# A second level of Strassen's algorithm in q, k and v, later sums of reciprocals, and another order of the output projection

## The chip, the core and the metric

The kernel runs on one core of a Trainium2 chip. The metric is the device time of one execution in microseconds (us), from runs of the compiled program; beside it stands one execution recorded by the hardware profiler. The engines are called by the profile's names: PE (TensorE, matmuls), PEld (its weight loads), DVE (VectorE), ACT (ScalarE), POOL (GpSimd) and SP (SyncE, which here issues the transfers).

## What is computed

Two graph layers over 64 items of 256 nodes with 512 features, all in float32. Layer 0 multiplies by the adjacency matrix and a weight; layer 1 is attention with 8 heads of 64 in which the adjacency matrix acts as a mask. Names and shapes of the arguments are shortened here:

```python
def setup_inputs(seed=0):
    x = -0.0003929 + 0.9999 * jax.random.normal(..., (64, 256, 512), jnp.float32)
    # adj [256, 256] f32: symmetric pattern with ones on the diagonal, times uniform(0.05, 1)

def _layernorm(x, axis=-1, eps=1e-5):
    m = jnp.mean(x, axis=axis, keepdims=True)
    v = jnp.var(x, axis=axis, keepdims=True)
    return (x - m) / jnp.sqrt(v + eps)

def reference(x, adj, L0_gnn_weight, L0_gnn_bias, Wq, bq, Wk, bk, Wv, bv, Wo, bo):
    h = jnp.maximum(_layernorm(x), 0.0)                       # layer 0
    y = jnp.einsum('nm,bmd->bnd', adj, h)
    x = x + jnp.einsum('bnd,do->bno', y, L0_gnn_weight) + L0_gnn_bias
    h = jnp.maximum(_layernorm(x), 0.0)                       # layer 1
    q = (h @ Wq + bq).reshape(b, n, 8, 64)                    # k and v alike
    scores = jnp.einsum('bqhd,bkhd->bhqk', q, k) / jnp.sqrt(64.)
    scores = scores + (1.0 - adj)[None, None, :, :] * -1000000000.0
    attn = jax.nn.softmax(scores, axis=-1)
    out = jnp.einsum('bhqk,bkhd->bqhd', attn, v).reshape(b, n, 512)
    return x + out @ Wo + bo
```

## The kernel before

**Groups and layers.** The 64 items are worked in 32 groups of two (GB = 2). Layer 0 runs over all groups first and leaves residual and hidden state in DRAM; layer 1 then runs over all groups again. Its steady loop has two halves per group g. First half: attention of heads 0 to 3 (`attend(g, 0)`), the scores of heads 4 to 7 (`score(g, 1)`), then the projections q and k of group g+1 (`queries_keys`). Second half: `attend(g, 1)`, `score(g+1, 0)`, then v of group g+1 (`values`) and the output projection of group g (`post`).

**Products.** Every projection has a weight of 512 x 512 and uses one level of Strassen's algorithm in Winograd's form, in `project`: seven products instead of eight, each of a 256 x 256 weight quarter and 256 tokens. The left factors are weight quarters a11, a12, a22 and prepared sums s1 to s4; the right factors are quarters b11, b21, b22 of the activations and their differences t1 to t4 (`Halves`, written by POOL). The products are called P1 = a11·b11, P2 = a12·b21, P3 = s4·b22, P4 = a22·t4, P5 = s1·t1, P6 = s2·t2, P7 = s3·t3. `product` (L439) issues four matmuls of 128 x 128 weights with 256 columns for each; where the activations are the weights (`by_token`, for v and o) the two sides are swapped. P1, P6 and P7 add up in one PSUM bank (a), P5 and P3 in another (c); between two products ACT (q, k, v) or DVE (o) reads the partial sum (`read`). P2 and P4 have banks of their own (b, d). A `finish` is one DVE addition of a bank and a partial sum (L493). The order is P1 P2 P6 P5 P7 P4 P3, and for the output projection of the last group P1 P5 P2 P6 P7 P4 P3. The partial sums that ACT leaves share three SBUF buffers (`partial`, tag u).

**Order of the work.** The program is written out by hand. Each engine works strictly in the order in which its instructions are written; a `yield` in a projection ends a step, `tick` (L263) counts steps, and `after(n, f)` writes f's instructions n steps later. PSUM has 8 banks, handed out by `bank` in the order in which they were given back (`give`); a bank's next writer waits until its last reader is done.

**Attention.** `score` (L684) makes four pairs of banks with scores, scaled and masked by DVE (L699), then POOL subtracts a maximum (L705), ACT takes the exponent (L710) a few steps later and POOL the sums over pairs of key tiles (L717). `attend` (L719) makes denominators (pden, L726) and weighted values (pav, L733) on PE, ACT copies the denominators (L740), DVE takes four reciprocals of 128 columns (L743) and, one step later in `divide`, multiplies (L750) and gives the banks back; ACT then sums the reciprocals over the free dimension into `stats` (L752), a check for overflow which is evaluated in the last group (L843 to L847). POOL makes the differences of the output projection (L437) in `divide`.

Of the kernel before, what the change touches and what calls it, by code (L numbers as in the profile page):

```python
# [8 lines left out]
F32 = mybir.dt.float32  # L9
# [4 lines left out]
P = 128  # L14
# [184 lines left out]
def kernel(  # L199
# [239 lines left out]
    def product(ps, s, a, halves, b, by_token, start=True, stop=True):  # L439
        for m in range(2):  # L440
            for c in range(2):
                w, y = s[a][:, c, :], halves.operand(b, c)
                lhs, rhs = (y[:, m * P:(m + 1) * P], w) if by_token else (w[:, m * P:(m + 1) * P], y)
                nc.tensor.matmul(ps[:, m, :], lhs, rhs, start=(start and m + c == 0), stop=(c == 1),  # L444
                                 skip_group_check=True)

    def project(s, halves, by_token, name, read, finish, first_half_first=False):


        def new(n):  # L450
            return bank([P, 2, N], f"{name}{n}")
        pa = new("a")
        product(pa, s, "a11", halves, "b11", by_token, stop=False)
        u1 = read(pa, 1)
        yield
        if first_half_first:
            pc = new("c")
            product(pc, s, "s1", halves, "t1", by_token, stop=False)
            c22 = read(pc, 0)
            yield  # L460
        pb = new("b")
        product(pb, s, "a12", halves, "b21", by_token)
        finish(pb, u1, 0, 0)
        give(pb)
# [4 lines left out]
        if not first_half_first:  # L469
            pc = new("c")  # L470
            product(pc, s, "s1", halves, "t1", by_token, stop=False)
            c22 = read(pc, 0)
            yield
        product(pa, s, "s3", halves, "t3", by_token, start=False)
        u3 = read(pa, 3)
        finish(pa, c22, 1, 1)
        give(pa)
        yield
        pd = new("d")
        product(pd, s, "a22", halves, "t4", by_token)  # L480
        finish(pd, u3, 1, 0)
        give(pd)
        yield
        product(pc, s, "s4", halves, "b22", by_token, start=False)
        finish(pc, u2, 0, 1)
        give(pc)
        yield

    def partial(name, n):
# [2 lines left out]
    def add(o, ps, u):  # L492
        nc.vector.tensor_tensor(o, ps, u, op=ALU.add)  # L493
# [125 lines left out]
    def hidden_sums(g, *steps):  # L619

        HH[g] = Halves(f"h_{g}", [H1T[g][:, k] for k in range(GB)], 0 if g else 1)
        for step, n in zip(steps, ("t1", "t2", "t3", "t4")):
            after(step, HH[g].sums, nc.gpsimd, (n,))

    def queries_keys(g):

        for n, store in (("q", Q), ("k", K)):
            store[g] = {}
            bias = L1[n][1]

            def read(ps, m):
                u = partial(f"{n}_{g}", m)
                for c in range(2):
                    f = 2 * (m in (0, 3)) + c
                    nc.scalar.activation(u[:, c, :], ps[:, c, :], AF.Identity, bias=bias[:, f:f + 1])
                return u

            def finish(ps, u, i, k):
                o = store[g][i, k] = act.tile([P, 2, N], F32, tag=f"{n}{i}{k}", name=f"{n}_{g}_{i}{k}")
                add(o, ps, u)  # L640

            yield from project(W[n], HH[g], False, f"{n}_{g}", read, finish)

    def values(g):
        v = act.tile([P, HQ, GB, NT, HF], F32, tag="yT0", name=f"v_{g}")
        V[g] = {(i, k): v[:, i, k] for i in range(HQ) for k in range(GB)}

        def read(ps, m):
            u = partial(f"v_{g}", m)
            nc.scalar.copy(u, ps)  # L650
            return u

        def finish(ps, u, i, k):
            add(V[g][i, k], ps, u)

        yield from project(W["v"], HH.pop(g), True, f"v_{g}", read, finish)

    def quarter_of(batch, i):
        return batch.rearrange("(t p) d -> p t d", p=P)[:, :, i * HF:(i + 1) * HF]
# [59 lines left out]
    def attend(g, qd):  # L719
# [19 lines left out]
        den, rden = dens[:, 0, :], dens[:, 1, :]  # L739
        nc.scalar.activation(den, pd, AF.Identity, accum_out=stats[:, 0, i:i + 1])  # L740
        give(pd)
        for c in range(4):
            nc.vector.reciprocal(rden[:, c * P:(c + 1) * P], den[:, c * P:(c + 1) * P])  # L743
# [140 lines left out]
```

## Time and profile before

| what | us |
|---|---|
| median of 3 runs | 2728.7 (2726.19 to 2729.91) |
| the profiled execution | 2727.19 |
| its span, first to last instruction | 2725.3 |
| one steady group of layer 1 (start of scores to the next, 1845.3 to 1910.25) | 64.95 |

In such a group the engines are busy for 64.95 (PE), 53.45 (PEld), 32.66 (DVE), 19.38 (ACT) and 43.26 us (POOL). The granted clock of PE is 0.998 of the full one over the execution. The page's groups of instructions that the change touches:

```profile
L743 DVE RECIPROCAL den<-den 128x128 f32<-128x128 f32 x256 | 216.8, 909 | 66.9 <-ACT den L740 66.8
L752 ACT ACTIVATE den<-den 128x512 f32<-128x512 f32 x64 | 40.3, 630 | 221.5 <-DVE den L743 221.5
```

A line gives the source line, engine, operation, output and inputs with partitions x elements, and the count; then the busy time in us and the mean of one in ns; then the idle time of the engine in front of them and what ended it. In front of the sums of L752, ACT is idle for 221.5 us in all, and DVE's reciprocals end that. PE's recorded lengths overlap, because matmuls are pipelined; its pace is read from start to start.

### The profile page before, as it was taken

The page shows a single profiled execution, that of the slowest core. Times are in us where ns is not written, and L with a number is a line of the kernel's source. Part 1 is how long each engine was busy: PE and PEld are TensorE (multiplying, and loading weights), DVE is VectorE, ACT ScalarE, POOL GpSimd, SP SyncE. Part 2 cuts the span into 40 slices and gives each one's busy share as a digit, 9 for nine tenths or more (in the row PEclk, how much of TensorE's full clock was granted, in tenths as well). Part 3 has the DMA queues.
Part 4 walks back from the last instruction along what each step waited for, and adds up shares of the span by engine and source line. Part 5 has one row for each costly group of instructions (what it writes and reads, how often), then busy time and mean ns, then how long its engine had stood idle before and what let it go on. Part 6 is the DMA issues. An engine that isn't in the chain of part 4 may idle for free.

```text
span 2725.3 us, 43511 instructions
## 1 busy us (share of the span) xinstructions
PE 2699.5 (99%) x17172; PEld 2252.1 (83%) x17172; DVE 1539.6 (56%) x2781; ACT 874.2 (32%) x1537; POOL 1823.1 (67%) x1426
## 2 busy tenths in 40 slices
PE   8999999999999999999999999999999999999998
PEld 7888888888788888888888888888888888888886
DVE  7877778775444444455554444454555445444556
ACT  3434343443233223222233322222223332223222
POOL 6777776764666666666666666666666666666665
PEclk9999999999999999999999999999999999999999
DMA  7776666664111111111111111111222111111110
GB/s 187 188 193 163 162 168 169 165 153 93 47 47 47 47 47 47 47 47 47 47 47 47 47 47 47 47 47 56 61 62 57 48 47 47 47 47 47 47 47 32
DMA packets 281023, 210.50 MB, mean 77 GB/s; under 512 B 145904, under 2 KB 212976, under 8 KB 280816
## 3 DMA queue, kind: packets, MB, share of 16 engines
q1 hardware_dynamic: 280352, 207.15, 29.2%
q8 instruction: 138, 2.26, 0.4%
q10 hardware_dynamic: 464, 0.52, 0.1%
q14 instruction: 69, 0.57, 0.1%
HBM read 106.96 MB, written 100.66 MB: 76 GB/s over the span
## 4 chain that ended last, share of the span: by engine, by line
PE 98%; POOL 1%; DVE 1%; DMA 0%; issue 0%; ACT 0%; DVEq 0%; ACTq 0%; POOLq 0%
PE sc L694 8%; PE py L539 8%; PE pav L733 8%; PE pden L726 2%; POOL a L705 1%; PE v_31a L444 0%; PE q_31a L444 0%; PE q_27a L444 0%; PE v_22a L444 0%; PE v_18a L444 0%; PE q_18a L444 0%; PE q_14a L444 0%; PE v_9a L444 0%; PE v_5a L444 0%; PE q_5a L444 0%; PE v_30a L444 0%
## 5 line engine op out<-in xcount | busy, mean ns | idle before, releaser
L705 POOL TENSOR_TENSOR a<-a,top 128x1024 f32<-128x1024 f32 x254 | 593.7, 2373 | 699.1 <-DVE a L699 699.1
L699 DVE SCALAR_TENSOR_TENSOR a<-sc,maskT 128x512 f32<-128x512 f32 x512 | 312.1, 683 | 28.5 <-PE sc L694 28.5
L717 POOL TENSOR_TENSOR as<-a 128x512 f32<-128x512 f32 x256 | 317.3, 1277 | 0.7 <-DVE r L575 0.7
L710 ACT ACTIVATE a<-a 128x1024 f32<-128x1024 f32 x256 | 270.8, 1058 | 22.4 <-POOL a L705 22.4
L743 DVE RECIPROCAL den<-den 128x128 f32<-128x128 f32 x256 | 216.8, 909 | 66.9 <-ACT den L740 66.8
L694 PE MATMUL sc<-q,k 64*128 64x256 f32 x2048 | 238.7, 383 | 0.0
L733 PE MATMUL pav<-a,v 128*32 128x256 f32 x4096 | 232.7, 379 | 0.0
L694 PEld LDWEIGHTS sc<-q,k 64*128 64x128 f32 x2048 | 194.4, 187 | 44.9 <-issue 26.3
L539 PE MATMUL py<-adjT,h 128*128 128x256 f32 x1024 | 228.9, 382 | 0.9 <-DVE adjT L325 0.9
L740 ACT ACTIVATE den<-pden 128x512 f32<-128x512 f32 x64 | 38.2, 597 | 581.7 <-PE pden L726 570.6
L539 PEld LDWEIGHTS py<-adjT,h 128*128 128x128 f32 x1024 | 196.1, 192 | 28.7 <-ACT h L514 1.2
L733 PEld LDWEIGHTS pav<-a,v 128*32 128x32 f32 x4096 | 133.1, 110 | 87.9
L569 ACT ACTIVATE h<-x,nb,rs 128x512 f32<-128x512 f32 x128 | 97.1, 806 | 319.0 <-POOL nb L54 319.0
L824 POOL TENSOR_TENSOR x<-x,bo_r 128x512 f32<-128x512 f32 x128 | 159.4, 1283 | 12.9 <-DVE x L493 12.9
L53 POOL TENSOR_TENSOR rs<-rs,mhalf 128x2 f32<-128x2 f32 (+1 forms) x97 | 78.8, 812 | 124.3 <-DVE nb L52 124.2
L518 POOL TENSOR_TENSOR x<-x,b_r 128x512 f32<-128x512 f32 x128 | 159.3, 1280 | 1.0 <-ACT h L514 0.9
L437 POOL TENSOR_TENSOR t_y<-yT,t_y 128x256 f32<-128x256 f32 (+1 forms) x96 | 87.8, 915 | 41.5 <-ACT yT L549 39.0
L752 ACT ACTIVATE den<-den 128x512 f32<-128x512 f32 x64 | 40.3, 630 | 221.5 <-DVE den L743 221.5
L590 DVE BATCH_NORM_STATS2 st<-x 128x6 f32<-128x256 f32 x256 | 96.4, 418 | 4.4
L514 ACT ACTIVATE h<-x,nb,rs 128x512 f32<-128x512 f32 x128 | 93.9, 805 | 10.5 <-POOL nb L54 10.5
L42 DVE BATCH_NORM_STATS2 st<-x 128x6 f32<-128x512 f32 x128 | 85.6, 669 | 7.2 <-DMA x<-in_x_dram 7.2
L437 POOL TENSOR_TENSOR t_y<-yT 128x256 f32<-128x256 f32 (+1 forms) x96 | 87.6, 912 | 2.2 <-ACT yT L549 0.9
(3144 smaller groups left out, 5550.1 us busy)
## 6 DMA issues: line engine op xcount, KB each, us to landing
x<-in_x_dram SPq DMA_DIRECT2D x256, 128.0 KB, 3.5
residual<-x SPq DMA_DIRECT2D x256, 128.0 KB, 2.3
hidden<-r SPq DMA_DIRECT2D x128, 256.0 KB, 4.7
h1T<-hidden SPq DMA_DIRECT2D x64, 512.0 KB, 9.5
x<-residual SPq DMA_DIRECT2D x32, 1024.0 KB, 6.5
out_dram<-x SPq DMA_DIRECT2D x62, 512.0 KB, 3.0
w_sb<-in_L_gnn_weight_dram SPq DMA_DIRECT2D x1, 1024.0 KB, 6.3
wq_sb<-in_L_gnn_Wq_dram SPq DMA_DIRECT2D x1, 1024.0 KB, 6.8
```

The costliest lines, as they stand in the source:

```text
L437: eng.tensor_tensor(self.t[n][:, c, :], self.operand(p, c), self.operand(q, c), op=ALU.subtract)
L518: nc.gpsimd.tensor_tensor(xt[:, t, :], xt[:, t, :], b0_r, op=ALU.add)
L539: nc.tensor.matmul(pss[d][:, b * N:(b + 1) * N], h[:, b * NT + k, d * P:(d + 1) * P], adjT[:, k, :], start=(k == 0), stop=(k == NT - 1))
L569: nc.scalar.activation(h1[:, k * NT + t, :], xt[:, k * NT + t, :], AF.Relu, bias=nb[:, t:t + 1], scale=rs[:, t:t + 1])
L694: nc.tensor.matmul(ps[j][:, kt * N:(kt + 1) * N], k[j * HD:(j + 1) * HD, c, kt * P:(kt + 1) * P], q[j * HD:(j + 1) * HD, c, :], start=True ...
L699: nc.vector.scalar_tensor_tensor(a[:, j * NT:(j + 1) * NT, :].rearrange("p k n -> p (k n)"), ps[j], SCALE, maskT_f, op0=ALU.mult, op1=ALU.add)
L705: nc.gpsimd.tensor_tensor(a, a, top_b, op=ALU.subtract)
L710: nc.scalar.activation(a, a, AF.Exp)
L717: nc.gpsimd.tensor_tensor(AS[c, b], a4[:, :, 0, :], a4[:, :, 1, :], op=ALU.add)
L733: nc.tensor.matmul(po[f][h * 32:(h + 1) * 32, b * N:(b + 1) * N], v[:, k, h * HD + f * 32:h * HD + f * 32 + 32], A[h // 2, b][:, (h % 2) * ...
L743: nc.vector.reciprocal(rden[:, c * P:(c + 1) * P], den[:, c * P:(c + 1) * P])
L824: after(9 + t, lambda t, xt: nc.gpsimd.tensor_tensor(xt[:, t, :], xt[:, t, :], L1["o"][1], op=ALU.add), t, X[g])
```

## The change

**Second level.** For groups 4 to 31 (`FIRST2 = 4`) q, k and v run through the new `project2`. P2, P3 and P4, whose result goes into one quarter of the output only, are split once more: `product2` computes each with seven matmuls of a 128 x 128 weight with 128 columns, four of them into the product's own bank and the common ones into a further bank (`shared`). `finish2` is a list of five DVE operations in place of one addition: own bank plus partial sum, then the shared parts added to 512, 384, 256 and 256 columns of the result (128 in the last, where the product had no earlier content in its bank, `fresh`). P3's and P2's finishes are issued in turn, after P2. The order is P1 P5 P6 P3 P2 P7 P4. P1, P5, P6 and P7 stay as they are.

**Its operands.** `block_sums` forms the sums of the weights' blocks, 12 POOL operations on 128 x 128 for each of q, k and v, in groups 0 to 2, in SBUF that layer 0 no longer needs. `block_hidden` forms the differences of the activations' blocks: six POOL operations per group, issued in the last steps of the second half.

**Reciprocals.** From group 4 on two of the four reciprocals are taken in `attend` and two one step later, at the head of `divide`; in the last `attend` all four stay. The sum of the reciprocals on ACT (`note`) is issued three steps after `divide`, except in the last group.

**Output projection.** It runs for all groups in the order P1 P5 P2 P6 P4 P7 P3 (`in_place=True`); there a partial sum is added to its quarter of x in place, so P4 needs no earlier partial sum. The output's transfers go out after P7 and P3; in the last group they go out by quarters, those that P4 and P7 complete together after P7.

The diff, with blank lines and parts of `project`'s rewritten steps left out:

```diff
@@ project and what is new beside it @@
-    def project(s, halves, by_token, name, read, finish, first_half_first=False):
+    def project(s, halves, by_token, name, read, finish, in_place=False):
+        def p1():
+            o["a"] = new("a")
+            product(o["a"], s, "a11", halves, "b11", by_token, stop=False)
+            o["u1"] = read(o["a"], 1)
...
+        def p3():
+            product(o["c"], s, "s4", halves, "b22", by_token, start=False)
+            finish(o["c"], o["u2"], 0, 1)
+            give(o["c"])
...
+            product(o["a"], s, "s3", halves, "t3", by_token, start=False)
+            o["u3"] = read(o["a"], 3)
+            finish(o["a"], o["c22"], 1, 1)
+            give(o["a"])
+        o = {}
+        for step in (p1, p5, p2, p6, p4, p7, p3) if in_place else (p1, p2, p6, p5, p7, p4, p3):
+            step()
+            yield
+    ONCE = {"a12": "b21", "a22": "t4", "s4": "b22"}
+    FIRST2 = 4
+    W2, spare = {}, []
+    def block_sums(n):
+        todo = []
+        for a in ONCE:
+            w = W[n][a]
+            def part(i, j):
+                return w[:, j, i * P:(i + 1) * P]
+            s1, s2, s3, s4 = (spare.pop(0) for _ in range(4))
+            W2[n, a] = dict(a11=part(0, 0), a12=part(0, 1), a22=part(1, 1), s1=s1, s2=s2, s3=s3, s4=s4)
+            for o, p, q, op in ((s1, part(1, 0), part(1, 1), ALU.add), (s2, s1, part(0, 0), ALU.subtract),
+                                (s3, part(0, 0), part(1, 0), ALU.subtract), (s4, part(0, 1), s2, ALU.subtract)):
+                todo.append((nc.gpsimd.tensor_tensor, o, p, q, op))
+        return todo
+    class Blocks:
+        def __init__(self, x, t):
+            self.x, self.t = x, t
+        def operand(self, n):
+            if n[0] == "t":
+                return self.t[..., {"t1": 0, "t3": 1, "t2": 2, "t4": 3}[n], :]
+            return self.x[..., int(n[1]) - 1, int(n[2]) - 1, :]
+        def sums(self, eng):
+            t, op = self.t, ALU.subtract
+            eng.tensor_tensor(t[..., 0:2, :], self.x[..., :, 1, :], self.x[..., 0, :, :], op=op)
+            eng.tensor_tensor(t[..., 2, :], self.operand("b22"), t[..., 0, :], op=op)
+            eng.tensor_tensor(t[..., 3, :], self.operand("b21"), t[..., 2, :], op=op)
+    def product2(own, shared, s, x, by_token, fresh):
+        q = own.rearrange("p m (n k) -> p (m n) k", k=P)
+        c11, c12, c21, c22 = (q[:, i, :] for i in ((0, 2, 1, 3) if by_token else (0, 1, 2, 3)))
+        for o, a, b, start in ((shared[:, 0, :], "a11", "b11", True), (shared[:, 1, :], "s2", "t2", False),
+                               (shared[:, 2, :], "s3", "t3", False),
+                               (c22 if fresh else shared[:, 3, :], "s1", "t1", fresh),
+                               (c11, "a12", "b21", False), (c12, "s4", "b22", False), (c21, "a22", "t4", False)):
+            lhs, rhs = s[a], x.operand(b)
+            if by_token:
+                lhs, rhs = rhs, lhs
+            nc.tensor.matmul(o, lhs, rhs, start=start, stop=True, skip_group_check=True)
+    def finish2(o, own, shared, u, by_token, fresh):
+        def quarters(t):
+            return t.rearrange("p m (n k) -> p (m n) k", k=P)
+        def spread(i, n):
+            return shared[:, i:i + 1, :].to_broadcast([P, n, P])
+        q = quarters(o)
+        lower = q[:, 1::2, :] if by_token else q[:, 2:4, :]
+        right = q[:, 2:4, :] if by_token else q[:, 1::2, :]
+        return [(o, own, u), (q, spread(0, 4), q), (q[:, 1:4, :], spread(1, 3), q[:, 1:4, :]),
+                (lower, spread(2, 2), lower),
+                (right[:, 0, :], quarters(own)[:, 3, :], right[:, 0, :]) if fresh else (right, spread(3, 2), right)]
+    def project2(n, halves, blocks, by_token, name, read, target):
+        s = W[n]
+        def new(i):
+            return bank([P, 2, N], f"{name}{i}")
+        def once(own, a, i, k, u, fresh):
+            shared = bank([P, 4, P], f"{name}r")
+            product2(own, shared, W2[n, a], blocks[ONCE[a]], by_token, fresh)
+            return own, shared, finish2(target(i, k), own, shared, u, by_token, fresh)
+        def finish_all(*products):
+            for ops in zip(*(ops for _, _, ops in products)):
+                for op in ops:
+                    add(*op)
+            for own, shared, _ in products:
+                give(own)
+                give(shared)
         pa = new("a")
         product(pa, s, "a11", halves, "b11", by_token, stop=False)
         u1 = read(pa, 1)
         yield
...
+        pc = new("c")
+        product(pc, s, "s1", halves, "t1", by_token, stop=False)
+        c22 = read(pc, 0)
         product(pa, s, "s2", halves, "t2", by_token, start=False, stop=False)
         u2 = read(pa, 2)
         yield
+        c12 = once(pc, "s4", 0, 1, u2, False)
+        yield
+        c11 = once(new("b"), "a12", 0, 0, u1, True)
+        finish_all(c12, c11)
+        yield
         product(pa, s, "s3", halves, "t3", by_token, start=False)
         u3 = read(pa, 3)
-        finish(pa, c22, 1, 1)
+        add(target(1, 1), pa, c22)
...
+        finish_all(once(new("d"), "a22", 1, 0, u3, True))
@@ beside queries_keys, values and post @@
+    H2 = {}
+    def block_hidden(g, step):
+        t = act.tile([P, GB, 4, P], F32, tag="t2", name=f"t2_{g}")
+        t4 = act.tile([P, 4, P], F32, tag="t24", name=f"t24_{g}")
+        x = H1T[g][:, :, 2:4, :].rearrange("p k c (n j) -> p k c n j", j=P)
+        both = Blocks(x, t)
+        last = Blocks(HH[g].t["t4"].rearrange("p c (n j) -> p c n j", j=P), t4)
+        H2[g] = {f"b2{k + 1}": Blocks(x[:, k], t[:, k]) for k in range(GB)}
+        H2[g]["t4"] = last
+        after(step, both.sums, nc.gpsimd)
+        after(step + 1, last.sums, nc.gpsimd)
...
+            def target(i, k):
+                o = store[g][i, k] = act.tile([P, 2, N], F32, tag=f"{n}{i}{k}", name=f"{n}_{g}_{i}{k}")
+                return o
...
+                add(target(i, k), ps, u)
+            if g < FIRST2:
+                yield from project(W[n], HH[g], False, f"{n}_{g}", read, finish)
+            else:
+                yield from project2(n, HH[g], H2[g], False, f"{n}_{g}", read, target)
...
-        yield from project(W["v"], HH.pop(g), True, f"v_{g}", read, finish)
+        if g < FIRST2:
+            yield from project(W["v"], HH.pop(g), True, f"v_{g}", read, finish)
+        else:
+            yield from project2("v", HH.pop(g), H2.pop(g), True, f"v_{g}", read, lambda i, k: V[g][i, k])
...
-        done = []
+        complete = {(0, 0): [(0, 0)], (1, 0): [], (1, 1): [(1, 0), (1, 1)], (0, 1): [(0, 1)]}
...
-            done.append(k)
             if g == NG - 1:
-                nc.sync.dma_start(quarter_of(out[g * GB + k], i), o)
-            elif done.count(k) == 2:
+                for i, k in complete[i, k]:
+                    nc.sync.dma_start(quarter_of(out[g * GB + k], i), quarter(xt, i, k))
+            elif (i, k) in ((1, 1), (0, 1)):
+                k = 1 - i
                 nc.sync.dma_start(out[g * GB + k].rearrange("(t p) d -> p t d", p=P), xt[:, k * NT:(k + 1) * NT, :])
-        yield from project(W["o"], halves, True, f"o_{g}", read, finish, first_half_first=g == NG - 1)
+        yield from project(W["o"], halves, True, f"o_{g}", read, finish, in_place=True)
@@ attend @@
-        for c in range(4):
+        def invert(c):
             nc.vector.reciprocal(rden[:, c * P:(c + 1) * P], den[:, c * P:(c + 1) * P])
+        early = 2 if g >= FIRST2 and (g, qd) != (NG - 1, 1) else 4
+        for c in range(early):
+            invert(c)
...
+        def note():
+            nc.scalar.activation(den, rden, AF.Identity, accum_out=stats[:, 1, i:i + 1])
         def divide():
+            for c in range(early, 4):
+                invert(c)
             for f in range(2):
                 nc.vector.tensor_tensor(OT[g][:, 2 * qd + f, :], po[f], rden, op=ALU.mult)
                 give(po[f])
-            nc.scalar.activation(den, rden, AF.Identity, accum_out=stats[:, 1, i:i + 1])
+            if g < NG - 1:
+                after(3, note)
+            else:
+                note()
@@ the main loop @@
+        if g == 0:
+            for n, tag in ((4 * DC, "w0_sb"), (4, "w0_s1"), (4, "w0_s2"), (4, "w0_s4"), (4, "adjT"), (4, "b0_r")):
+                t = const.tile([P, n, P], F32, tag=tag, name=f"spare_{tag}")
+                spare.extend(t[:, i, :] for i in range(n))
+        if g < 3:
+            for i, work in enumerate(block_sums("qkv"[g])):
+                after(4 + i // 2, *work)
...
                 hidden_sums(g + 2, 2, 3, 4, 5)
+                if g + 2 >= FIRST2:
+                    block_hidden(g + 2, 6)
```

More of the change, by code (lines that the diff above doesn't have):

```diff
@@ L445, in product, with p2, p4, p5 @@
                                  skip_group_check=True)
-    def project(s, halves, by_token, name, read, finish, first_half_first=False):
+    def project(s, halves, by_token, name, read, finish, in_place=False):
         def new(n):
             return bank([P, 2, N], f"{name}{n}")
+        def p1():
+            o["a"] = new("a")
+            product(o["a"], s, "a11", halves, "b11", by_token, stop=False)
+            o["u1"] = read(o["a"], 1)
+        def p2():
+            pb = new("b")
+            product(pb, s, "a12", halves, "b21", by_token)
+            finish(pb, o["u1"], 0, 0)
+            give(pb)
+        def p3():
+            product(o["c"], s, "s4", halves, "b22", by_token, start=False)
+            finish(o["c"], o["u2"], 0, 1)
+            give(o["c"])
+        def p4():
+            pd = new("d")
+            product(pd, s, "a22", halves, "t4", by_token)
+            finish(pd, o.get("u3"), 1, 0)
+            give(pd)
+        def p5():
+            o["c"] = new("c")
+            product(o["c"], s, "s1", halves, "t1", by_token, stop=False)
+            o["c22"] = read(o["c"], 0)
+        def p6():
+            product(o["a"], s, "s2", halves, "t2", by_token, start=False, stop=False)
+            o["u2"] = read(o["a"], 2)
+        def p7():
+            product(o["a"], s, "s3", halves, "t3", by_token, start=False)
[6 more added lines that the diff above has]
+            yield
@@ L455, in project @@
         yield
[L456 to L464, printed above, removed]
+        pc = new("c")
+        product(pc, s, "s1", halves, "t1", by_token, stop=False)
+        c22 = read(pc, 0)
         yield
@@ L468, in project @@
         yield
[L469 to L473, printed above, removed]
+        c12 = once(pc, "s4", 0, 1, u2, False)
[3 more added lines that the diff above has]
+        yield
         product(pa, s, "s3", halves, "t3", by_token, start=False)
         u3 = read(pa, 3)
-        finish(pa, c22, 1, 1)
+        add(target(1, 1), pa, c22)
         give(pa)
         yield
[L479 to L486, printed above, removed]
+        finish_all(once(new("d"), "a22", 1, 0, u3, True))
         yield
@@ L636, in read @@
                 return u
+            def target(i, k):
+                o = store[g][i, k] = act.tile([P, 2, N], F32, tag=f"{n}{i}{k}", name=f"{n}_{g}_{i}{k}")
+                return o
             def finish(ps, u, i, k):
-                o = store[g][i, k] = act.tile([P, 2, N], F32, tag=f"{n}{i}{k}", name=f"{n}_{g}_{i}{k}")
-                add(o, ps, u)
-            yield from project(W[n], HH[g], False, f"{n}_{g}", read, finish)
+                add(target(i, k), ps, u)
[3 more added lines that the diff above has]
+                yield from project2(n, HH[g], H2[g], False, f"{n}_{g}", read, target)
     def values(g):
```

## The prediction

> **What bounds the kernel now.** I read the page's busy line and its shares of the chain of waits first, then the waits of PE, then the timeline of one steady group of layer 1.
>
> ```profile
> PE 2699.5 (99%) x17172; PEld 2252.1 (83%) x17172; DVE 1539.6 (56%) x2781; ACT 874.2 (32%) x1537; POOL 1823.1 (67%) x1426
> ...
> PE 98%; POOL 1%; DVE 1%; DMA 0%; issue 0%; ACT 0%; DVEq 0%; ACTq 0%; POOLq 0%
> ```
>
> PE is busy for 2699.5 of 2725.3 us and is 98% of the chain that ended last. All waits of PE add up to 20.8 us (9.5 and 0.9 at the start, 2.4 in group 1, 4.5 and 3.2 in the last group, 0.3). Between groups 2 and 30 none is listed: there only less PE work, or a new wait, changes the time.
>
> ```profile
> 1871.48 1.89 PE L444 MATMUL k_19c<-h1T,wk_s 128*128 128x256 f32 x8
> 1873.30 1.07 PE L726 MATMUL pden<-as,ones 128*32 128x256 f32 x16
> 1874.18 3.64 PE L733 MATMUL pav<-a,v 128*32 128x256 f32 x64
> 1877.75 3.73 PE L694 MATMUL sc<-q,k 64*128 64x256 f32 x32
> 1881.40 1.99 PE L444 MATMUL v_19a<-wv_sb,h1T 128*128 128x256 f32 x8
> ```
>
> The columns are start, length, engine, line, operation, tiles, shapes, count. What counts is start to start, since the recorded lengths overlap. From q_19a (1855.94) to k_19c (1871.48) nine products take 15.54 us: 1.727 us each, 216 ns for each of 8 records (a 128x256 f32 matmul leaves two records, each with a weight load of its own). A group takes 64.95 us.
>
> **PE: the second level.** In groups 4 to 31, q, k and v each do three of their seven products as seven blocks: 28 x 9 = 252 products. Four matmuls with 256 columns become seven with 128, so 8 records become 14, each with half the columns and a full weight load. Half of 216 ns is 108 ns, so the gain is one eighth, if the weight loads keep up. No f32 product with 128 columns is in the trace; the nearest row is the four transposes of the mask, with 128 columns and a fresh 128x128 load each:
>
> ```profile
> 416.96 0.60 PE L341 MATMUL pm<-ident,adj_sb 128*128 128x128 f32 x4
> 417.39 0.38 PE L539 MATMUL py<-adjT,h 128*128 128x256 f32 x1
> ...
> L341 PEld LDWEIGHTS pm<-ident,adj_sb x4: 141/142/142, 416.7 to 417.2; 128*128 128x128 f32 x4
> L444 PEld LDWEIGHTS w_0a<-w_sb,yT x8: 190/190/190, 20.8 to 22.3; 128*128 128x128 f32 x8
> ```
>
> Four records in 417.39 - 416.96 = 0.43 us: 107.5 ns each, although each load is recorded at 141 ns (the last two lines give min/median/max in ns). So a load's record is longer than what it holds up. But a product's load is recorded at 190, 49 longer, and may hold up more. Two rows speak to that. The score matmuls put a 128-column load (187 ns) in front of every record and run 32 of them in 3.65 us, 114 ns each; they alternate between two halves of the array, so this is weaker. And after the scores, where v_19a's first load is not hidden, v_19a to v_19b takes 1883.23 - 1881.40 = 1.83 us, only 0.10 above 1.727: a bare load costs some 100 ns, not 190. The ends are 107.5 (transposes) and 190 (the load's record). I take **109**, at the near row, as the three rows agree. 14 x 109 = 1.526 us; saved 0.201 us a product, 1.81 us a group, **50.6 us** in all. Each ns of spacing is worth 14 x 252 ns = 3.5 us, and the gain is gone at 1727/14 = 123.3 ns.
>
> One rule of the Trainium skill speaks against this: "TensorE: Matmul & The Clock Gate", section "Back-to-back issue gap", says that a stream of pairs of load and matmul at 128 columns runs at about 81 ns, not at the bare 56, since the load takes a share. Laid on our records (an estimate), 109 + 25 = 134 ns: 14 x 134 = 1.876 us, a loss of 0.149 x 252 = 38 us. The same page (Part 3, "What overlaps and what doesn't") lets loads overlap only across different row groups. Against the second stands every product here: eight full-array loads of 190 ns hide in 1.727 us. Against the first stand the transposes' 107.5, though only four of them. I go with the rows and keep the rule as the slower rival.
>
> **VectorE: what the saving is paid with.** One add of a bank (690 ns recorded, 0.60 us from start to start: two take 1.29) becomes five operations. Between 128x512 (0.68) and 128x1024 (1.22) the slope is 1.04 ns a column, so 384, 256 and 128 columns are 0.47, 0.33 and 0.20 us (estimates). A block product finishes in 0.60 + 0.60 + 0.47 + 0.33 + 0.20 = 2.20 us, or 2.33 for s4·b22: about +1.65 x 252 = 416 us of DVE work, which takes it from 56% to 73%. None of it is on the path while DVE stays ahead of PE. The tight stretch, in us from the start of the scores that precede q: P1 of q starts at 3.65, a full product is 1.727, a block one 1.526, so k's P2 ends at 23.37, k's P4 at 26.62, and the next scores start 4.54 later (1877.75 - 1873.21, the end of k_19c), at 31.16. DVE can start on them 1.23 us in, at 32.39:
>
> ```profile
> 1873.40 0.69 DVE L493 TENSOR_TENSOR k<-k_19c,u_k 128x512 f32<-128x512 f32 x1 [1.03 <-PE k_19c L444]
> 1875.15 3.39 DVE L743 RECIPROCAL den<-den 128x128 f32<-128x128 f32 x4 [1.06 <-ACT den L740]
> 1878.98 4.88 DVE L699 SCALAR_TENSOR_TENSOR a<-sc,maskT 128x512 f32<-128x512 f32 x8 [0.44 <-PE sc L694]
> ```
>
> DVE starts 0.19 after P2 ends, at 23.56; nine operations (3.93; the first of s4·b22's is done before) to 27.49; P7's add to 28.09; P4's five to 30.29; two reciprocals (2 x 0.85) to 31.99: 0.40 us to spare. With four it would be 33.69, 1.3 late: this is what moving two of them behind the scores buys. Five dependent operations in a row can cost more: bad to worst (L843, L844) shows 0.04 after the record's end, so 0.13 per step, 0.52 over P4's, which eats the spare. The scores' fourth pair of banks reuses the first pair's, so PE feels a delay only beyond about 0.2. I charge **0.15 us a group, +4 us**; ends 0 and 0.9 (DVE's 8.4 us of work 10% longer), 25 us in all.
>
> The other half of a group: v's last finish ends near 19, the read of o's P1 near 20.0, and o's P6, which adds to that bank, now starts fourth, at 15.14 + 3 x 1.727 = 20.32. In the old place, third (18.59), it would wait 1.4. So the **new order** is cover for the longer finishes, worth nothing by itself. The later reciprocals put oT 1.8 us later (9.1 instead of 7.3), but Pool, its reader, is at its subtractions until 11.9.
>
> **ScalarE.** The sum of reciprocals waits 3.5 us for DVE each time (221.5 us over 63). With half the reciprocals later it would hold up P1's read in the strict queue of ACT; three steps later it stands behind an exponent. Cost 0: ACT is busy for 19.4 of 64.95 us.
>
> **Pool.** Per group three sums of 512, 256 and 256 columns and three of 256, 128 and 128: by 1.24 us for 512 and 2.33 for 1024, about 4.2 us. They come last in the half, after 25.6; Pool is idle until the next scores (12.2 and 9.5 us before the subtractions): hidden. The 36 weight blocks in groups 0 to 2 (about 0.4 us each) delay the key sums by some 4 us; those ended 10 us before attention. Queues: the number of transfers and their places on SP stay (the output leaves after the sixth and seventh product, as before), Pool issues none.
>
> **The last group.**
>
> ```profile
> 2683.13 1.89 PE L444 MATMUL o_30b<-wo_sb,oT 128*128 128x256 f32 x8
> 2689.55 3.54 PE L444 MATMUL o_30a<-wo_s,t_o 128*128 128x256 f32 x8 [4.54 <-POOL t_o L437]
> ```
>
> The 4.54 us wait is for t2, now in fourth place: 1.7 us shorter, and the product behind it, which ran at 3.38 us instead of 1.73, may stay fast. Late next is t4 (0.5 us). Two late reciprocals of group 31 push DVE's last chain back by 1.7 us. Together -1 (from -3 to +2).
>
> **Sum**, against the profiled execution's 2727.2 (span 2725.3 and 1.9 around it): 2727.2 - 50.6 + 4 - 1 = **2680**. The median of the runs is 1.5 higher, within the range.
>
> **Rivals.** (a) *VectorE becomes the bound* around the scores and between q and k. For it: 8.4 us of work for 9.0 us of PE. Against it: only the excess over the spare counts, and DVE has 6 us a half to catch up. 0.9 us a group: **2705**; from 0.5 on, above 2692. (b) *The weight load sets the pace* of the 128-column records, slower than before: one mechanism, in the 252 block products, decided at 123.3 ns. For it: the 190 ns record and the rule above; against it: transposes and bare load. At 134 ns 2680 + 88 = **2768**, at 141 ns 2793. (c) *The change doesn't do what it says*: a spacing of about 122 with DVE hidden, seven small matmuls no cheaper than four large: 2727.
>
> **How the numbers follow.** Forecast 2668 to 2692: 62%. Better still (107.5 ns, no stall): 4%. (a), 2692 to 2722: 20%. (c), within 0.2% (5.5 us, about what a measurement can tell from no change): 4%. (b): 10%. Faster 0.86, same 0.04, slower 0.10. Low: 107.5 gives 14 x 107.5 = 1.505, saved 0.222 x 252 = 56, and -3 at the end: 2668; I say 2666. High: 2712 takes in most of (a), which leaves about 0.18 outside.
>
> **What would show it.** Right: records of 128x128 products 108 to 110 ns apart; about 63.2 us per group from group 4 on; PE without waits in those groups; DVE near 73%; groups 0 to 3 and layer 0 as before. Wrong: products of 1.7 us or more at seven matmuls; PE waiting for DVE at the scores or at q's and k's P6; five-step finishes of 2.7 us and more.

## The result, and the profile after it

| | before | after |
|---|---|---|
| median of the runs, us | 2728.99 (4 runs, 2726.19 to 2729.91) | 2688.65 (4 runs, 2688.09 to 2690.02) |
| span of the profiled execution, us | 2725.3 | 2686.3 |
| one steady group of layer 1, us | 64.95 | 63.49 |

The ratio is 0.9855 (95% interval 0.9838 to 0.9872). The forecast was 2680, with 2666 to 2712 around it: the time fell by 40.3 us where 47.6 had been forecast. The page of the changed kernel, busy time and chain:

```profile
PE 2659.3 (99%) x18684; PEld 2267.5 (84%) x18684; DVE 1958.6 (73%) x3789; ACT 868.9 (32%) x1537; POOL 1960.1 (73%) x1630
...
PE 97%; DVE 1%; POOL 1%; DMA 0%; issue 0%; SPq 0%; ACTq 0%; POOLq 0%; DVEq 0%
```

PE is still the chain. DVE stands at 73%, as forecast. All of PE's waits, in us in all, times, longest:

```profile
PE pa L323 <- DVE adj_p L318: 9.8, 1, 9.8
PE pf L1009 <- DVE worst L1007: 3.8, 1, 3.8
PE o_30a L444 <- POOL t_o L437: 2.8, 1, 2.8
PE q_1a L444 <- POOL t_h L437: 2.4, 1, 2.4
PE py L655 <- DVE adjT L325: 0.9, 1, 0.9
PE o_31b L444 <- DVE oT L901: 0.8, 1, 0.8
PE sc L835 <- DVE a L840: 0.6, 1, 0.6
PE o_30d L444 <- POOL t_o L437: 0.5, 1, 0.5
```

The waits of the o products belong to the last two groups. Before them, from group 4 on, there is one wait: 0.6 us at the scores after k of group 4. (They stand behind `attend(3, 1)`, and group 3 still takes four reciprocals early.) The gain is therefore to be read from PE's pace. P3 and P2 of q of group 19 run between the first two of these lines of PE's timeline, P4 from the third to the last:

```profile
1832.13 0.39 PE L545 MATMUL q_19r<-h1T,wq_s 128*128 128x128 f32 x2
...
1835.26 1.89 PE L444 MATMUL q_19a<-t_h,wq_sb 128*128 128x256 f32 x8
1836.99 0.38 PE L545 MATMUL q_19r<-t_h,wq_sb 128*128 128x128 f32 x2
...
1837.66 0.39 PE L545 MATMUL q_19d<-t,spare_w_sb 128*128 128x128 f32 x2
...
1838.55 0.38 PE L444 MATMUL k_19a<-h1T,wk_sb 128*128 128x256 f32 x1
```

P4's fourteen records (r is the bank of the common parts, d the product's own) take 1838.55 - 1836.99 = 1.56 us; the 28 of P3 and P2 take 1835.26 - 1832.13 = 3.13 us. Together that is **111.7 ns a record**, 1.564 us a product, 0.163 us less than 1.727. Nine products make 1.47 us a group, and the period fell by 1.46.

Where the 39.0 us of span went, by the starts of the same work in both traces:

| stretch | before | after | difference |
|---|---|---|---|
| start to the scores in front of q of group 4 | 870.56 | 869.48 | -1.1 |
| from there to the last scores | 1807.08 | 1766.94 | -40.1 |
| from the last scores to the end | 47.66 | 49.88 | +2.2 |

252 x 0.163 = 41.1 us less PE's work and about 1.4 more for group 3's one wait (the run with four early reciprocals below shows what such a wait costs) give the -40 of the middle row. The first row holds layer 0 and groups 0 to 3, which have no second level. This stretch takes 869.2 to 871.0 us in the traces of the changed kernel and of its first six variants below, so 1.1 us is no more than its spread.

### The profile page after: what moved, and what is told of

Same layout as the page of the kernel before. It is cut to its first block, busy times and chain, and to the rows that moved or that the text cites. A ratio compares the mean times of both kernels' runs of the same rounds, so it can differ in the third digit from the quotient of the medians.

```text
span 2686.3 us, 47911 instructions
## 1 busy us (share of the span) xinstructions
PE 2659.3 (99%) x18684; PEld 2267.5 (84%) x18684; DVE 1958.6 (73%) x3789; ACT 868.9 (32%) x1537; POOL 1960.1 (73%) x1630
## 4 chain that ended last, share of the span: by engine, by line
PE 97%; DVE 1%; POOL 1%; DMA 0%; issue 0%; SPq 0%; ACTq 0%; POOLq 0%; DVEq 0%
PE sc L835 8%; PE py L655 8%; PE pav L874 8%; PE pden L867 2%; POOL a L846 1%; DVE v L609 0%; DVE k L609 0%; PE v_29a L444 0%; PE q_29a L444 0%; PE v_28a L444 0%; PE v_27a L444 0%; PE v_25a L444 0%; PE q_25a L444 0%; PE v_24a L444 0%; PE q_23a L444 0%; PE q_21a L444 0%
## 5 line engine op out<-in xcount | busy, mean ns | idle before, releaser
L851 ACT ACTIVATE a<-a 128x1024 f32<-128x1024 f32 x256 | 264.1, 1054 | 22.4 <-POOL a L846 22.4
L885 DVE RECIPROCAL den<-den 128x128 f32<-128x128 f32 x256 | 223.7, 919 | 38.0 <-ACT den L881 37.9
L691 DVE STREAM_TRANSPOSE r<-h 128x512 f32<-128x512 f32 x128 | 82.7, 683 | 2.1 <-ACT h L685 1.4
```

The lines of the kernel that those rows point to most:

```text
L851: nc.scalar.activation(a, a, AF.Exp)
```

## The experiments

Each is an edit of the changed kernel, but for the first. The times are medians; the kernel before ran beside them at 2728.5 to 2728.8.

**What sets the spacing of 128-column records.** A kernel of its own; its core:

```python
            nc.tensor.matmul(o, w[:, i % 4, (i // 4 % 3) * P:(i // 4 % 3) * P + loaded], t[:, (i + 1) % 4, :columns],
                             start=(i == 0), stop=(i == records - 1), skip_group_check=True)
```

> A kernel of its own: bursts of 24 f32 matmuls (48 records) on PE, each with a weight load of its own, then a copy of x to the output; it computes none of the reference. Moving columns 256, 192, 160, 128, 96, 64 with 128 loaded columns, then 128 moving columns with 96, 64 and 32 loaded. Theory W, the weight load sets the pace of the 128-column records (111.7 ns in the changed kernel): the spacing is 216, 162 and 136 ns at 256, 192 and 160 columns, stays at about 112 ns at 128, 96 and 64 columns, and at 128 moving columns falls to 108 or 109 when 96 or fewer columns are loaded. Theory M, each record has a fixed cost beside its columns: 85 ns at 96 and 58 ns at 64 moving columns, and 111.7 ns at 128 moving columns whatever is loaded.

The timeline of PE. The bursts whole and cols_a to cols_e have 256, 192, 160, 128, 96 and 64 moving columns with 128 loaded ones; load_a to load_c have 128 moving columns with 96, 64 and 32 loaded ones. The first four lines are whole bursts of 48 records, the other four the inside of a burst without its first and last records:

```profile
32.15 10.52 PE L34 MATMUL ps_whole<-t,w 128*128 128x256 f32 x48
42.51 7.96 PE L34 MATMUL ps_cols_a<-t,w 128*128 128x192 f32 x48
50.31 6.68 PE L34 MATMUL ps_cols_b<-t,w 128*128 128x160 f32 x48
56.83 5.52 PE L34 MATMUL ps_cols_c<-t,w 128*128 128x128 f32 x48
...
57.05 5.08 PE L34 MATMUL ps_cols_c<-t,w 128*128 128x128 f32 x44
67.83 4.85 PE L34 MATMUL ps_cols_e<-t,w 128*128 128x64 f32 x42
83.60 4.97 PE L34 MATMUL ps_load_a<-t,w 128*96 128x128 f32 x44
94.34 4.97 PE L34 MATMUL ps_load_c<-t,w 128*32 128x128 f32 x44
```

The granted clock is 1.00 over all these bursts. From one start to the next over 48 records, the spacing shrinks with the moving columns: 215.8, 162.5 and 135.8 ns at 256, 192 and 160. Inside a burst, the length of the last record (275 ns, or 273 in the last two lines) is taken off, and the rest is divided by one less than the count. With 128 loaded columns that is (5.08 - 0.275)/43 = 111.7 ns at 128 moving columns and, within the rounding of a timeline, the same at 64. Taken singly from the trace, the records at 128, 96 and 64 moving columns lie 111 or 112 ns apart, 111.7 on average: a floor that does not depend on the moving columns. With 128 moving columns and 96, 64 or 32 loaded ones the spacing is (4.97 - 0.273)/43 = 109.2 ns in each of the three bursts, where theory W had 108 or 109.

Two things follow. The floor goes when fewer columns are loaded, while the count of instructions and the moving columns stay, so it is the load's and not a fixed cost of each record. Theory M, with 85 and 58 ns at 96 and 64 moving columns, fails. And 109.2 ns is the matmul's own pace at 128 columns: it lies on the line of 215.8, 162.5 and 135.8, which loses 26.7 ns for every 32 columns. A load of 128 f32 columns holds the records at 111.7 ns, 2.5 more than their matmuls need.

The Trainium skill's "TensorE: Matmul & The Clock Gate", section "LDWEIGHTS (loading the stationary operand)", gives the columns over 1.2 GHz, 107 ns for 128; measured is 5 more. These 5 ns decide here: at 107 ns the load would stay behind the 109.2 of its matmul (an estimate from that section's figure), and the saving would be some 50 us, as forecast.

**Four early reciprocals.**

```diff
-        early = 2 if g >= FIRST2 and (g, qd) != (NG - 1, 1) else 4
+        early = 4
```

> The changed kernel with all four reciprocals in attend, as before the change. Theory: DVE comes to the scores after k with nothing to spare (reciprocals end at 1855.90, the first score operation starts at 1855.93), two more reciprocals take 1.75 us, PE's fourth pair of banks forgives 0.28: 1.4 us of waiting of PE for DVE at the scores, once in each of 28 groups, +40 us: about 2728. Rival: the scores' banks and DVE's idle time later in the half take it up: 2689, within 3.

Measured: 2727.1 us, ratio to before 0.9995 (0.9987 to 1.0004). PE's timeline shows the place, and DVE's the cause:

```profile
1486.75 2.86 PE L835 MATMUL sc<-q,k 64*128 64x256 f32 x24
1490.18 1.72 PE L835 MATMUL sc<-q,k 64*128 64x256 f32 x8 [0.57 <-DVE a L840]
...
1486.20 3.38 DVE L885 RECIPROCAL den<-den 128x128 f32<-128x128 f32 x4
```

The 32 records of the scores break before the fourth pair of banks, once a group, and the period is 64.92 us instead of 63.49: 1.43 more. Only 0.57 of it is recorded as a wait, because the records overlap; by their starts, the first 24 and the gap behind them take 3.43 us, 0.7 more than 24 records at the 114 ns of an undisturbed row, and the last eight another 0.7 more. This one detail takes back the whole gain.

**P6 of the output projection in third place.**

```diff
-        for step in (p1, p5, p2, p6, p4, p7, p3) if in_place else (p1, p2, p6, p5, p7, p4, p3):
+        for step in (p1, p2, p6, p5, p4, p7, p3) if in_place else (p1, p2, p6, p5, p7, p4, p3):
```

> The changed kernel with P6 of the output projection back in third place (P1 P2 P6 P5 P4 P7 P3). Theory: DVE's read of o's P1 ends at 1874.73 behind v's finish, P6 in third place would start at 1873.50: PE waits 1.3 us in each of 28 groups, and 1.7 us more for t2 in the last: about 2727. Rival: the order alone is worth only the last group: 2690.

Measured: 2733.5 us, ratio 1.002 (1.0013 to 1.0027). PE waits at P6 for DVE's read of P1 (the second DVE line), which stands behind v's finishes (the first):

```profile
1442.34 0.28 DVE L609 TENSOR_TENSOR v<-v_12d,v 128x128 f32<-128x128 f32 x1
1442.54 0.68 DVE L609 TENSOR_TENSOR x<-o_11a,x 128x512 f32<-128x512 f32 x1
...
1443.37 1.97 PE L444 MATMUL o_11a<-wo_s,t_o 128*128 128x256 f32 x8 [1.21 <-DVE x L609]
```

The period is 64.93 us, 1.44 more; PE's list has this wait 27 times, 39 us in all. The stretch behind the last scores adds 5 (its waits for t2 and oT are 1.7 us longer each, and the product behind the first is slow again), so the 38 expected were some 7 too few.

**The sum of the reciprocals at once.**

```diff
-            if g < NG - 1:
-                after(3, note)
-            else:
-                note()
+            note()
```

> The changed kernel with the sum of the reciprocals on ACT issued in divide, as before the change, the reciprocals still two and two. Theory: ACT is held until the last reciprocal (1830.97), then sums for 0.8 us, and only then reads P1; P6, which adds to the same bank, waits 2.3 us in the half with q and 2.0 in the half with v: 28 x 4.3 = +120 us, about 2809. Rival: ACT, idle for two thirds of the time, takes it up: 2689, within 3.

Measured: 2817.4 us, ratio 1.0327 (1.031 to 1.0345). Timelines of PE and ACT:

```profile
1417.92 1.89 PE L444 MATMUL q_12c<-t_h,wq_s 128*128 128x256 f32 x8
1421.91 1.97 PE L444 MATMUL q_12a<-t_h,wq_s 128*128 128x256 f32 x8 [2.09 <-ACT u_q L765]
...
1420.31 0.63 ACT L895 ACTIVATE den<-den 128x512 f32<-128x512 f32 x1 [10.50 <-DVE den L885]
1420.94 0.82 ACT L765 ACTIVATE u_q<-q_12a,bq_c 128x256 f32<-128x256 f32 x2
```

ACT had been idle for 10.5 us, but in front of a sum that waited for DVE; the read of P1 stood behind it, and PE behind that. The period is 67.83 us, 4.34 more (4.3 expected); PE's list has 27 waits in the half with q and 27 in the half with v, some 117 us. The span grew by 129. The other 12 are a second effect, which the theory left out: in seven groups the period is 69.52, 1.69 more, and in each of these the profile grants PE half its clock for 3.41 us behind the wait, for the first time at 1011.53. The last section comes back to this.

**The other parts without the second level.**

```diff
-    FIRST2 = 4
+    FIRST2 = 99
...
-        if g < 3:
+        if False:
             for i, work in enumerate(block_sums("qkv"[g])):
```

> The changed kernel without the second level (no group uses it, no block sums): what is left is the later sum of the reciprocals and the new order of the output projection, with four early reciprocals. Theory: the saving is the second level's alone; the rest acts only in the last group, where P6 waits 1.7 us less for t2 and the product behind it keeps its pace (1.65 us less): 2725 to 2728, 1 to 3 below before. Rival: the order or the later sum brings part of the 40 us in every group: below 2720.

Measured: 2726.8 us, ratio 0.9994 (0.9986 to 1.0003), 2.0 below before; the period is 64.96. The wait for t2 is 2.82 us instead of 4.54, and the product behind it runs at its pace. So order and later sum save nothing by themselves in a steady group; the two runs before show that the second level needs both to keep what it saves.

**All early in the last group.**

```diff
-        early = 2 if g >= FIRST2 and (g, qd) != (NG - 1, 1) else 4
+        early = 2 if FIRST2 <= g < NG - 1 else 4
```

> The changed kernel with all four reciprocals taken early in both attentions of the last group instead of the last only. Theory: the chain at the end of the program runs through DVE (late reciprocals, oT, differences, the reads of x, the overflow check), so 1.75 us of DVE's work leave it and P2's wait of 0.77 for oT goes: 2686.5, 2.2 below the changed kernel. Rival: PE's and Pool's own chain sets the end: no change, 2688.6.

Measured: 2687.9 us, 0.7 below the changed kernel, within its spread: a miss. P2's wait for oT went and the check's fell to 3.16 us, but the last scores now wait:

```profile
2639.93 1.72 PE L835 MATMUL sc<-q,k 64*128 64x256 f32 x8 [0.57 <-DVE a L840]
```

`attend(31, 0)` follows v's finishes with no output projection between, so there too DVE comes late to the scores. The end of the chain did what was expected: from the first product of the last projection to the check's matmul it is 10.33 us instead of 12.20. I had looked only there.

**The overflow check later.**

```diff
     nc.vector.tensor_reduce(worst, bad, AX.X, ALU.max)
+    run(last, 2)
     pf = bank([1, 1], "pf")
```

> The changed kernel with the overflow check's matmul issued after the sixth product of the last projection instead of the fourth; the two DVE operations in front of it stay where they are. Theory: PE, which waits 3.80 us at this matmul and then runs P4 and P7 at a reduced pace (3.58 and 2.40 instead of 1.73), goes on with P4, P7 can start when DVE has read P6 (2672.4 instead of 2676.55): about 4 us less, 2684.5. Rival: DVE's and Pool's chain sets the end anyway, within 1 of 2688.6.

Measured: 2685.2 us, 3.4 below the changed kernel (4 expected). In the changed kernel's timeline the last products run like this:

```profile
2672.85 0.19 PE L1009 MATMUL pf<-ones,worst 128*1 128x1 f32 x2 [3.80 <-DVE worst L1007]
2672.97 3.78 PE L444 MATMUL o_31d<-wo_sb,t_o 128*128 128x256 f32 x8
2676.55 2.57 PE L444 MATMUL o_31a<-wo_sb,t_o 128*128 128x256 f32 x8
```

Start to start P4 takes 3.58 us and P7 2.40, instead of 1.73, after 3.80 us of idling; the granted clock is 0.50 from 2671.08 to 2677.91. With the check later, P4 starts at 2670.80, the clock stays at 1.00 and both run at their pace; P7 waits 1.08 for DVE's read of P6.

**Shorter finishes with four early reciprocals.**

```diff
-        return [(o, own, u), (q, spread(0, 4), q), (q[:, 1:4, :], spread(1, 3), q[:, 1:4, :]),
+        every = [(o, own, u), (q, spread(0, 4), q), (q[:, 1:4, :], spread(1, 3), q[:, 1:4, :]),
...
+        return every[:2]
...
-        early = 2 if g >= FIRST2 and (g, qd) != (NG - 1, 1) else 4
+        early = 4
```

> Four early reciprocals as in the earlier run, and of each block product's five finishing operations only the first two: the blocks of q, k and v stay incomplete. Theory: the 40 us of the early reciprocals are DVE's time before the scores; the dropped operations take 3.1 us out of the stretch after k's P2, more than the 1.75 that the reciprocals add, so the wait at the scores goes and the time is that of the changed kernel, 2688.6 within 3 (PE's pace, the weight loads, does the rest). Rival: the early reciprocals cost PE in another way: about 2727 as in that run.

Measured: 2685.4 us, no wait at the scores, period 63.5:

```profile
1853.01 3.72 PE L836 MATMUL sc<-q,k 64*128 64x256 f32 x32
...
1850.41 3.39 DVE L886 RECIPROCAL den<-den 128x128 f32<-128x128 f32 x4 [0.33 <-ACT den L882]
1854.24 4.88 DVE L841 SCALAR_TENSOR_TENSOR a<-sc,maskT 128x512 f32<-128x512 f32 x8 [0.44 <-PE sc L836]
```

With DVE's time taken out, the four early reciprocals cost nothing: DVE is done with them before the scores and waits 0.44 us for PE. PE's pace stays where the loads hold it. It is 3.2 below the changed kernel: 1.4 is group 3's wait, which goes too; in the last group P2's wait for oT goes (0.77), and the check's falls from 3.80 to 3.15 us.

**Together.**

```diff
-    FIRST2 = 4
+    FIRST2 = {"q": 2, "k": 3, "v": 3}
...
-            if g < FIRST2:
+            if g < FIRST2[n]:
...
-        if g < FIRST2:
+        if g < FIRST2["v"]:
...
-        early = 2 if g >= FIRST2 and (g, qd) != (NG - 1, 1) else 4
+        early = 2 if g >= 1 and (g, qd) != (NG - 1, 1) else 4
...
-            after(9 + t, lambda t, xt: nc.gpsimd.tensor_tensor(xt[:, t, :], xt[:, t, :], L1["o"][1], op=ALU.add), t, X[g])
+            after(9 + t if g < NG - 1 else 7, lambda t, xt: nc.gpsimd.tensor_tensor(xt[:, t, :], xt[:, t, :], L1["o"][1], op=ALU.add), t, X[g])
...
+    run(last, 2)
     pf = bank([1, 1], "pf")
```

> The changed kernel with what the runs point to: the second level from group 2 for q and from group 3 for k and v (12 more block products, 12 x 0.163 = 2.0 us); two early reciprocals already from group 1 on, so that the one wait at the scores of group 3 goes (1.4 us); the overflow check's matmul after the sixth product (3.4 us, as in its own run); Pool's bias additions of the last group three steps and more earlier, so that DVE's reads of x do not wait for them and DVE's difference beside them (1.75 us instead of 0.69) is fast again (2.4 us). Theory: these add, 2688.6 - 9.2 = 2679.4. Rival: the earlier bias additions delay the key sums or t2 of group 30 on Pool, and PE's wait for t2 grows: 2683 or more.

Measured: **2679.7 us** (2678.87 to 2680.58), ratio to before 0.982 (0.9807 to 0.9834), 9.0 below the changed kernel: faster than both. The wait at the scores and the check's are gone from PE's list; t2's 2.8 us in group 30 remains. By the traces, the earlier second level and reciprocals bring 3.4 us (2.0 + 1.4 expected) and the stretch behind the last scores 5.1 (3.4 + 2.4 expected). There one DVE instruction changed its length, the first line in the changed kernel, the second here:

```profile
2667.52 1.75 DVE L437 TENSOR_TENSOR t_o<-oT,t_o 128x512 f32<-128x512 f32 x1
...
2666.03 0.68 DVE L437 TENSOR_TENSOR t_o<-oT,t_o 128x512 f32<-128x512 f32 x1
```

The first runs beside Pool's bias additions (from 2667.08), the second after they are done.

## Why the prediction was right, and where it was not

**What bounds the kernel, and that PE's work is the gain:** right. 2726.8 without the second level and 2688.65 with it are the change; DVE, at 73%, does not set the pace. The time lies in the band that was given 62%.

**The spacing of the records:** the term that was mis-sized. I put it at 109 ns, measured are 111.7, and at 3.5 us per ns the gain is 41.1 instead of 50.6 us. The sign that was named for being right, 108 to 110 ns, failed. The burst run shows which step was wrong: 109.2 ns is what a 128-column matmul takes by itself, so the figure was right for the matmul; wrong was that the load before it stays hidden. None of the three rows could show that. The transposes, the near row, have shorter loads (141 ns recorded, a product's 190), which I had seen and set aside; taken singly their records lie 109 ns apart (the 107.5 of the working is the rounding of a timeline), so they show the matmul's pace and not a product's load. The scores' loads alternate between halves of the array, and the bare load's some 100 ns came from a difference of two rounded starts. The rule that I weighed, laid on as 134 ns, missed by more and forecast a loss, but its reason was right: the load takes its share, here as soon as the matmul's own pace (109.2) is faster than the load's (111.7).

**DVE at the scores:** 4 us were charged, 0.15 a group. The changed kernel's timeline of DVE:

```profile
1851.58 0.68 DVE L609 TENSOR_TENSOR k<-k_19d,u_k 128x512 f32<-128x512 f32 x1
...
1853.95 0.28 DVE L609 TENSOR_TENSOR k<-k_19d,k 128x128 f32<-128x128 f32 x1
1854.15 1.75 DVE L885 RECIPROCAL den<-den 128x128 f32<-128x128 f32 x2
1855.93 4.87 DVE L840 SCALAR_TENSOR_TENSOR a<-sc,maskT 128x512 f32<-128x512 f32 x8
```

P4's five operations take 1851.58 to 1854.15, 2.57 us (2.20 to 2.72 in the working). The reciprocals end at 1855.90, and the first scores are ready 1.23 us after their start at 1854.69, at 1855.92: nothing to spare, and nothing lost. What was paid instead is one wait, about 1.4 us, where group 3 with its four early reciprocals meets the longer finishes of group 4; the working had not named it. That one more us of DVE would be felt at once, the first rival, is shown by the run with four early reciprocals: 1.75 us more cost 1.43. (That rival's sum, 2705, lays its 25 us on top of the 4 that 2680 already holds; 2701 was meant.)

**The order as cover:** right; 1.4 us were worked out, 1.44 measured. **ACT's sum:** right to call it necessary; the prediction gave it no price, and undone it is the dearest part of all, 4.34 us a group. **Pool:** right, hidden; its six sums end at 1884.96 (4.65 us for the 4.2 worked out), and its next work, the subtractions, starts at 1889.29.

**The last group:** -1 was forecast, +2.2 measured. The gain at t2 came (2.8 instead of 4.54, the pace kept): 2.5 us. The late reciprocals came, 1.9 us up to the check's matmul. Left out was PE's clock: the check's wait grew from 3.16 to 3.80 us, the granted clock fell to half before it ended, which it had not done in the kernel before, and the two products behind it took 2.5 us longer. That the pace was kept at t2 is in part luck, as the last section shows.

In sum: 9.5 too much on the spacing, 2.6 too much charged for the scores, 3.2 too little at the end, and 1.1 that the first stretch was shorter in this execution: 9.5 - 2.6 + 3.2 - 1.1 = 9.0; the profiled executions give 8.6 (39.0 less span, where 47.6 had been forecast). So a part of the closeness is that the unneeded charge of 4 us stood against the spacing.

## What to carry to other kernels

Splitting matmuls into smaller ones gains while the new number of records times their new spacing is less than before. The spacing is the larger of two paces, the matmul's and that of the load in front of it: measure both, the load's with a burst of fewer moving columns, since the profile's length of a load is not its pace. When an engine beside the bound one goes from 56% to 73%, its share of the time says little; work out the stretch between its last input and the next deadline, operation by operation, and move what can wait behind the deadline. On an engine with a strict order an instruction that waits costs more than one that works.

## What the runs showed of the hardware beyond that

- The f32 weight load has a pace of its own: 111.7 ns with 128 columns, whether 128, 96 or 64 columns move. With 96, 64 or 32 loaded columns it is hidden behind a 128-column matmul, at 109.2 ns. The profile records 192, 163, 137 and 110 ns for these loads.
- A DVE operation with two inputs in SBUF took 1.75 us beside Pool's additions, and 0.68 without them; DVE's reads of PSUM beside the same additions stayed at 0.68 or 0.69. "SBUF — State Buffer", section "Who interferes with whom", of the Trainium skill states that a DVE instruction with two SBUF inputs contends with a Pool instruction that reads SBUF, for a pair of ports that they share; the two rows agree with it. Of the 2.4 us expected from the earlier additions, this is 1.07; another 1.09 are two waits of DVE's reads of x for the additions (0.56 and 0.53 in the changed kernel), which the last run no longer has.
- PE's granted clock falls to half, and products then run at half pace (3.58 us for P4 behind the check instead of 1.73), in stretches of 3.41 us that lie on a fixed grid. In the run with the sum of the reciprocals at once, the seven steady groups that lose 1.69 us have such a stretch; the seven start 273.07 us apart, 80 times 3.413. Whether a wait sets one off depends on how it falls on the grid. These are three stretches each around PE's wait for t2, 2.83 us long in both, in the changed kernel and in the run with all reciprocals early in the last group (stretch, its length, time in which PE is busy, granted clock, share of DMA, GB/s):

```profile
2643.78:2647.19 3.41, 1.74 (x9) 1.00 0.00 0
2647.19:2650.60 3.41, 1.99 (x8) 1.00 0.02 5
2650.60:2654.01 3.41, 3.19 (x15) 1.00 0.00 0
...
2643.99:2647.40 3.41, 3.04 (x15) 1.00 0.00 0
2647.40:2650.81 3.41, 0.95 (x4) 1.00 0.00 0
2650.81:2654.22 3.41, 3.41 (x9) 0.50 0.03 5
```

In the first trace the wait is divided between two stretches, in each of which PE idles for about half; in the second most of it falls into one, where PE idles for 0.72, and the next stretch runs at half clock. Eight of the kept traces have this wait of 2.8 us; in four of them a stretch at half clock follows it, in four, the changed kernel's among them, none.

  Laid over all traces of this kernel and its variants from 20 us on, with PE's idle time as the profile records it: a stretch at full clock in which PE idled for 0.60 or more was followed by one at half clock each time (28 cases), and one with 0.57 or less never; in between, at 0.58, both occur. How long the clock then stays at half (one stretch, or two as behind the changed kernel's check) was not worked out. Where the grid lies in the program differs from execution to execution, so with waits of 2 to 4 us it is in part chance whether 1.7 us are lost behind them, and the parts of the last group are known no better than that.
